# SiLU as one ScalarE function in a bottleneck-attention layer: Identity, Tanh and a VectorE product replaced, with table loads called for in advance

## The chip, the cores and the metric

The kernel runs on one core of a Trainium2 chip. The metric is the device time of one execution in microseconds (us). Five engines work side by side and wait for one another through semaphores: TensorE (PE in the profile, its weight loads on a line PEld), VectorE (DVE), ScalarE (ACT), GpSimd (POOL) and SyncE (SP), the last used here for DMA issue alone.

## The reference, cut to what matters

The input is x, 8 images of 512 channels and 32x32 pixels, float32. F = 32 is the side, C = 256, two bottlenecks (N = 2), 4 heads of 64.

```python
def cbs(x, w, p, pad):                       # convolution, batch norm, SiLU
    return silu(bn_eval(conv2d(x, w, pad), p))

t = cbs(gn(x), cv1_w, cv1_bn, 0)             # 512 -> 512 channels
ys = [t[:, :C], t[:, C:]]
for i in range(N):
    yi = ys[-1]
    z = cbs(yi, m_cv1_w[i], m_cv1_bn[i], 1)  # 3x3, 256 -> 256
    z = bot_attention(z, m_qkv_w[i], m_rw[i], m_rh[i])   # softmax(q (k+r)) v
    z = silu(bn_eval(conv2d(z, m_cv2_w[i], 0), m_cv2_bn[i]))
    ys.append(yi + z)
return x + cbs(concat(ys), cv2_w, cv2_bn, 0) # 1024 -> 512
```

gn is a group norm over 32 groups. silu(u) = u / (1 + exp(-u)). With h = u/2 that is h (1 + tanh h).

## The kernel before, in words

All 8 images are worked through by a loop that is written out (b = 0 to 7). A tile holds 128 channels (partitions) by 1024 pixels, and most instructions work on a half, 128x512. The framework lists the instructions of each engine in an order that follows the program text where nothing else decides, and each engine then takes its list strictly in that order. `tc.issue_after(ins)` only puts what its block creates on the engine of `ins` behind `ins` in that list.

One image has these stages, with the helper that does each:

- `cv1` (L652): four output tiles `oc`, each the product of 4 channel tiles, and SiLU of each half (L658). Two tiles go to `ypad`, the padded input of the 3x3 convolution, two to `y0`. For all images but the first this stage is done during the image before: the two `ypad` tiles by `first` and `second` (L809, L815) at the end of attention 0, the two `y0` tiles (L823) behind `m2`.
- `tiles_in` (L277): VectorE turns `ypad` into 6 sets of transformed tiles `v_in` (3 pairs of rows by 2 channel tiles; the last instruction of a set is L330).
- `conv3x3` (L660): for each of 2 output tiles, 3 groups of products on TensorE (L674), then `columns_out` (L334: one ScalarE copy into a tile with tag `h`, four VectorE instructions), `rows_out` (L343) and SiLU in place of the two halves of `z` (L684).
- `project` (L421): q, k and v from `z` (L272, L449), ScalarE copies of q (L435) and v (L454).
- `attention_fast` (L459): per group of 64 x 2 heads and half image, logits (L483), Exp on ScalarE (L487), sums on VectorE (L490, L492) and the product with v (L506); then ScalarE's copy L513 and VectorE's addition L514. A group's sums of exponentials (L523) are copied by ScalarE (L530) into tiles with the tags `h` and `t`. There are 8 Exps of 128x1024 in a group, 4 groups, 16 attentions.
- `m2` (L687): the second 1x1 product (L693), SiLU of four halves and the residual addition (L701) into `ypad[N]` or, in the second bottleneck, into `ylast`.
- `cv2` (L714): four output tiles of 8 channel tiles each, SiLU of 8 halves, the addition of x (L738) and the DMA of the result (L740), from a tile with tag `t`.

SiLU is made by `silu_parts` (L254): ScalarE's Identity takes the PSUM tile with a scale and a bias per channel into `h` (L258), ScalarE's Tanh takes `h` into `t` (L259), and VectorE multiplies (L264, L700 or L737 by the caller):

```python
nc.scalar.activation(h, ps, AF.Identity, scale=sh[:, k : k + 1], bias=bh[:, k : k + 1])
nc.scalar.activation(t, h, AF.Tanh)
nc.vector.scalar_tensor_tensor(dst, t, 1.0, h, ALU.add, ALU.mult)
```

The tags `h` and `t` have two buffers each; products go to a PSUM pool `big` with three. The scale `sh` and bias `bh` hold half of the batch norm's factors, so that h is u/2. Of the whole kernel 256 SiLU halves are made so. Weights of the 3x3 convolution are transformed during image 0 (`make_u`, L202, on VectorE and ScalarE) and read back from DRAM for the others (`load_u`). At the end a value decides whether a general version of the whole runs again (L873); with these inputs it does not.

Of the kernel before, what the change touches and what calls it, by code (L numbers as in the profile page):

```python
# [36 lines left out]
F32 = mybir.dt.float32  # L40
I32 = mybir.dt.int32
AF = mybir.ActivationFunctionType
ALU = mybir.AluOpType
# [4 lines left out]
P = 128  # L48
# [8 lines left out]
def kernel(  # L57
# [16 lines left out]
    nc = tc.nc  # L74
# [8 lines left out]
    HALF = 512  # L83
    NH = HW // HALF
    ROWS = HALF // F
    SCALE = HD**-0.5
# [4 lines left out]
    const = ctx.enter_context(tc.tile_pool(name="const", bufs=1))  # L91
    fast = ctx.enter_context(ExitStack())
    act = fast.enter_context(tc.tile_pool(name="act", bufs=1))
# [30 lines left out]
    def bn_slot(src, n):  # L124
        at = len(bn_chunks)
        for c in range(n):
            bn_chunks.append(src[ts(c, P), :])
        return at

    bn_cv1 = bn_slot(cv1_bn, NX)  # L130
    bn_m1 = [bn_slot(m_cv1_bn[n], NM) for n in range(N)]
    bn_m2 = [bn_slot(m_cv2_bn[n], NM) for n in range(N)]
    bn_cv2 = bn_slot(cv2_bn, NO)
    NBN = len(bn_chunks)
    bnp = const.tile([P, NBN, 4], F32, name="bnp")
# [42 lines left out]
        ypad.append(yp)  # L178


    sh = const.tile([P, NBN], F32, name="sh")
    bh = const.tile([P, NBN], F32, name="bh")
    rstd = const.tile([P, NBN], F32, name="rstd")
    nc.vector.tensor_scalar(rstd, bnp[:, :, 3], BN_EPS, None, ALU.add)
    nc.gpsimd.tensor_tensor(rstd, rstd, mhalf[:, :NBN], ALU.pow)
    nc.vector.scalar_tensor_tensor(sh, bnp[:, :, 0], 0.5, rstd, ALU.mult, ALU.mult)
    nc.vector.tensor_tensor(bh, bnp[:, :, 2], sh, ALU.mult)
    nc.vector.scalar_tensor_tensor(bh, bnp[:, :, 1], 0.5, bh, ALU.mult, ALU.subtract)

    for at in bn_m1:  # L190
        nc.vector.tensor_scalar(sh[:, at : at + NM], sh[:, at : at + NM], 1 / 48, None, ALU.mult)
# [56 lines left out]
    def inner(yp, c, half):  # L248
        return yp[:, c, 1 + half * ROWS : 1 + (half + 1) * ROWS, :].rearrange("p h w -> p (h w)")

    def stages(act, small, ps_big, ps_av, n_pt):


        def silu_parts(ps, k):  # L254

            h = act.tile([P, HALF], F32, tag="h", name="h", bufs=2)
            t = act.tile([P, HALF], F32, tag="t", name="t", bufs=2)
            nc.scalar.activation(h, ps, AF.Identity, scale=sh[:, k : k + 1], bias=bh[:, k : k + 1])  # L258
            nc.scalar.activation(t, h, AF.Tanh)  # L259
            return h, t  # L260

        def silu(dst, ps, k):
            h, t = silu_parts(ps, k)
            nc.vector.scalar_tensor_tensor(dst, t, 1.0, h, ALU.add, ALU.mult)  # L264

        def conv1x1(w_of, rhs_of, nk, ks=None, ps=None):

# [191 lines left out]
        def attention_fast(n, z, at, behind):  # L459
# [9 lines left out]
            pairs = [steps[i : i + PAIR] for i in range(0, len(steps), PAIR)]  # L469
            pts, accs, avs = {}, {}, {}  # L470

            def logits(pair):
                g, j0 = pair[0]
                c, half = groups[g]
                pt = act.tile([P, PAIR, 2, HALF], F32, tag="pt", name="pt", bufs=n_pt)
                pts[pair[0]] = pt
                for i, (_, j) in enumerate(pair):
                    ps = ps_big.tile([P, 2, HALF], F32, tag="big", name="l_ps")
                    for hd in range(2):
                        r = slice(hd * HD, (hd + 1) * HD)  # L480
                        for kh in range(2):
                            o = j * P + kh * HD
                            nc.tensor.matmul(  # L483
                                ps[kh * HD : (kh + 1) * HD, hd, :], kr[r, c, o : o + HD],
                                q[r, c, ts(half, HALF)], start=True, stop=True,
                            )
                    nc.scalar.activation(pt[:, i], ps, AF.Exp, scale=SCALE)  # L487
                if j0 == 0:
                    accs[g] = act.tile([P, 2, HALF], F32, tag="acc", name="acc", bufs=2)
                    return nc.vector.tensor_tensor(accs[g], pt[:, 0], pt[:, 1], ALU.add)  # L490
                for i in range(PAIR):
                    ins = nc.vector.tensor_tensor(accs[g], accs[g], pt[:, i], ALU.add)  # L492
                return ins
# [92 lines left out]
            ps, rows, s_dram = sums(g)  # L586
# [73 lines left out]
        def conv3x3(n, vs, u_of):  # L660
            z = act.tile([P, NM, HW], F32, tag="z", name="z")
            for oc in range(NM):
                us = u_of(oc)
                r = act.tile([P, 2, 2, NT * NW, 2], F32, tag="acc", name="r_mid", bufs=2)
                ends = act.tile([P, 2, NT * NW, 2], F32, tag="rs", name="r_ends", bufs=2)
                rs = (r[:, 0], r[:, 1], ends)
                flat = [a.rearrange("p r q o -> p r (q o)") for a in rs]
                first, last = rows_out(z[:, oc, :], *flat)
                for i in range(PAIRS):
                    ps = ps_big.tile([P, 2, NC, NT * NW], F32, tag="big", name="c3_ps")  # L670
                    for row in range(2):
                        for col in range(NC):
                            for k in range(NM):
                                nc.tensor.matmul(  # L674
                                    ps[:, row, col, :], us[i][:, k, row, col, :], vs[i][:, k, row, col, :],
                                    start=(k == 0), stop=(k == NM - 1),
                                )
                    columns_out(rs[i], ps)
                    if i == 1:
                        first()  # L680
                last()
                for half in range(NH):
                    part = z[:, oc, ts(half, HALF)]
                    silu(part, part, bn_m1[n] + oc)  # L684
            return z

        def m2(n, ao, yi, dst_of):  # L687

            pss = [ps_big.tile([P, NH, HALF], F32, tag="big", name="m2_ps") for _ in range(NM)]
            for half in range(NH):  # L690
                for oc in range(NM):
                    for k in range(NM):
                        nc.tensor.matmul(  # L693
                            pss[oc][:, half, :], m2_sb[:, n, k, ts(oc, P)], ao[:, k, ts(half, HALF)],
                            start=(k == 0), stop=(k == NM - 1),
                        )
            for half in range(NH):
                for oc in range(NM):
                    h, t = silu_parts(pss[oc][:, half, :], bn_m2[n] + oc)
                    nc.vector.scalar_tensor_tensor(t, t, 1.0, h, ALU.add, ALU.mult)  # L700
                    last = nc.vector.tensor_tensor(dst_of(oc, half), t, inner(yi, oc, half), ALU.add)  # L701
            return last

# [10 lines left out]
        def cv2(b, w2, ys, begun=None):  # L714


            def rows_of(dram, oc, half):
                if isinstance(b, int):
                    return dram[b, ts(oc, P), ts(half, HALF)]
                return dram[bass.ds(b, 1), ts(oc, P), ts(half, HALF)][0]  # L720

            def residual(oc, half):
                t = act.tile([P, HALF], F32, tag="xr", name="x_res", bufs=2)
                nc.gpsimd.dma_start(t, rows_of(x, oc, half))
                return t

            pieces = [(oc, half) for oc in range(NO) for half in range(NH)]
            res = [residual(*pieces[0]), residual(*pieces[1])]
            for i, (oc, half) in enumerate(pieces):
                if half == 0:  # L730
                    ks = range((2 + N) * NM)
                    if i == 0 and begun is not None:
                        ps = cv2_products(w2, ys, oc, ks[-NM:], begun)
                    else:
                        ps = cv2_products(w2, ys, oc, ks)
                h, t = silu_parts(ps[:, half, :], bn_cv2 + oc)
                nc.vector.scalar_tensor_tensor(t, t, 1.0, h, ALU.add, ALU.mult)  # L737
                nc.vector.tensor_tensor(t, t, res.pop(0), ALU.add)  # L738
                q = nc.sync if isinstance(b, int) and i + 2 >= len(pieces) and b == B - 1 else nc.gpsimd
                q.dma_start(rows_of(out, oc, half), t)  # L740
                if i + 2 < len(pieces):
                    res.append(residual(*pieces[i + 2]))
# [28 lines left out]
    for b in range(B):  # L771
# [3 lines left out]
        def u_of(n):  # L775
            def of(oc):
                if b == 0 and (oc, 0) not in us:
                    make_all(n, oc)
                return [us.pop((oc, i)) if (oc, i) in us else load_u(n, oc, i) for i in range(PAIRS)]

            return of
# [27 lines left out]
        def first():  # L809
            nonlocal nxt  # L810
            if more:
                nxt = new_y0()
                s.cv1(w1, xs, nxt, y1n, Y1S[: NM // 2])
# [133 lines left out]
```

## Time and profile before

| | us |
|---|---|
| median of 3 runs | 2662.72 (2661.3 to 2666.34) |
| the profiled execution's own time | 2659.74 |
| its span, from the first to the last instruction | 2658.2 |
| TensorE busy in it | 2469.9 |

The span is the time the rows below are counted in. The rest of the execution's own time, 1.54 us, lies around it. In a row of the timeline the first number is the start in us from the span's start, the second the length; xN means N instructions merged in one row; the brackets give the idle time of the engine before the row and what ended it.

### The profile page before, as it was taken

The numbers are of one execution on the slowest core, as the hardware profiler recorded it, in microseconds if no ns is written. First come the engines' busy times: TensorE is split into PE (matmuls) and PEld (weight loads), VectorE is DVE, ScalarE is ACT, GpSimd is POOL, SyncE is SP. The second block draws the span as 40 slices with busy tenths as digits, with TensorE's granted clock in tenths as the row PEclk, the third lists the DMA queues.
The fourth block names the chain that finished last, engine by engine and source line by source line (L and its number), as shares of the span: only waits on it lengthen the run. The fifth ranks groups of instructions, "written<-read, shape, count | busy, mean of one in ns | idle before, by whom it ended". The sixth has DMA issues, their size and how long they took to land. (4 is left out here: it accounts for less than half of the span.)

```text
span 2658.2 us, 36654 instructions
## 1 busy us (share of the span) xinstructions
PE 2469.9 (93%) x14626; PEld 1230.8 (46%) x14626; DVE 1673.7 (63%) x2780; ACT 1059.6 (40%) x1513; POOL 114.6 (4%) x378
## 2 busy tenths in 40 slices
PE   6788999989999899999999989999999999999798
PEld 3425436354463634536354353634536354363533
DVE  6678564775656665666665665657666675646753
ACT  2354432535234352353524434244442534325252
POOL 2000000000100001000010000100001000010000
PEclk9899999999999999999999999999999999999999
DMA  6123104040130302203031130502205011050101
GB/s 215 62 79 107 66 24 176 14 143 10 51 144 14 143 14 85 106 14 143 14 133 62 30 123 14 188 7 71 82 14 190 10 68 53 10 190 14 48 14 57
DMA packets 86195, 199.43 MB, mean 75 GB/s; under 512 B 32384, under 2 KB 42112, under 8 KB 73728
## 3 DMA queue, kind: packets, MB, share of 16 engines
q1 hardware_dynamic: 73696, 151.35, 16.6%
q0 software_dynamic: 12320, 45.66, 4.8%
q8 instruction: 117, 1.92, 0.3%
q14 instruction: 62, 0.51, 0.1%
HBM read 166.89 MB, written 30.08 MB: 74 GB/s over the span
## 5 line engine op out<-in xcount | busy, mean ns | idle before, releaser
L487 ACT ACTIVATE pt<-l_ps 128x1024 f32<-128x1024 f32 x512 | 496.3, 1025 | 228.7 <-PE l_ps L483 228.7
L492 DVE TENSOR_TENSOR acc<-acc,pt 128x1024 f32<-128x1024 f32 x384 | 469.8, 1223 | 147.6 <-ACT pt L487 123.8
L506 PE MATMUL av_ps<-pt,vT 64*64 64x512 f32 x4096 | 492.6, 596 | 12.3 <-DVE ao L514 10.9
L483 PE MATMUL l_ps<-q,kr 64*64 64x512 f32 x4096 | 498.4, 603 | 4.3 <-ACT pt L487 4.3
L674 PE MATMUL c_ps<-v_in,u 128*128 128x128 f32 x2688 | 313.6, 280 | 37.0 <-DVE v_in L330 27.5
L674 PEld LDWEIGHTS c_ps<-v_in,u 128*128 128x128 f32 x2688 | 310.8, 196 | 46.6 <-DVE v_in L330 30.0
L506 PEld LDWEIGHTS av_ps<-pt,vT 64*64 64x64 f32 x4096 | 155.1, 135 | 313.4 <-issue 227.3
L483 PEld LDWEIGHTS l_ps<-q,kr 64*64 64x64 f32 x4096 | 156.1, 135 | 290.5 <-issue 268.5
L272 PE MATMUL ps<-z,qkv_sb 128*128 128x512 f32 x512 | 245.5, 630 | 43.1 <-DVE z L264 43.1
L258 ACT ACTIVATE h<-ps,bh,sh 128x512 f32<-128x512 f32 x128 | 93.5, 774 | 367.6 <-PE ps L272 268.5
L272 PE MATMUL ps<-x,w 128*128 128x512 f32 x512 | 228.0, 602 | 2.2 <-DVE x L406 2.2
L272 PE MATMUL ps<-ypad,w 128*128 128x512 f32 x512 | 227.1, 594 | 0.0
L272 PEld LDWEIGHTS ps<-z,qkv_sb 128*128 128x128 f32 x512 | 100.6, 202 | 159.4 <-issue 103.4
L490 DVE TENSOR_TENSOR acc<-pt 128x1024 f32<-128x1024 f32 x64 | 78.4, 1225 | 138.4 <-ACT pt L487 138.4
L259 ACT ACTIVATE t<-h 128x512 f32<-128x512 f32 x256 | 149.7, 622 | 32.2 <-DMA out_dram<-t 24.2
L440 DVE TENSOR_TENSOR kr<-ps,rw_sb 128x512 f32<-128x512 f32 x64 | 41.2, 686 | 186.0 <-PE ps L272 186.0
L272 PEld LDWEIGHTS ps<-x,w 128*128 128x128 f32 x512 | 97.2, 192 | 130.9 <-issue 126.9
L272 PEld LDWEIGHTS ps<-ypad,w 128*128 128x128 f32 x512 | 96.6, 190 | 125.1 <-issue 125.1
L337 ACT COPY m<-c_ps 128x256 f32<-128x256 f32 x96 | 35.8, 373 | 243.1 <-PE c_ps L674 224.2
L737 DVE SCALAR_TENSOR_TENSOR t<-t,h 128x512 f32<-128x512 f32 x64 | 43.4, 695 | 139.7 <-ACT t L259 139.7
L530 ACT COPY s_row<-s_ps 128x512 f32<-128x512 f32 x128 | 68.7, 589 | 151.2 <-PE s_ps L523 148.7
L272 PE MATMUL ps<-ylast,w 128*128 128x512 f32 x256 | 117.2, 595 | 10.5 <-DVE ylast L701 10.5
(119 smaller groups left out, 2342.8 us busy)
## 6 DMA issues: line engine op xcount, KB each, us to landing
u<-u SPq DMA_DIRECT2D x84, 1024.0 KB
w<-in_cv_w_dram SPq DMA_DIRECT2D x24, 1024.0 KB
x<-in_x_dram SPq DMA_DIRECT2D x32, 512.0 KB
x_res<-in_x_dram POOLq DMA_DIRECT2D x64, 256.0 KB, 3.9
out_dram<-t POOLq DMA_DIRECT2D x62, 256.0 KB, 3.4
u<-u_new POOLq DMA_DIRECT2D x12, 1024.0 KB, 5.2
rs<-r_dram SPq DMA_DIRECT2D x96, 128.0 KB
raw<-in_m_cv_w_dram SPq DMA_DIRECT2D x8, 576.0 KB
```

The costliest lines, as they stand in the source:

```text
L258: nc.scalar.activation(h, ps, AF.Identity, scale=sh[:, k : k + 1], bias=bh[:, k : k + 1])
L259: nc.scalar.activation(t, h, AF.Tanh)
L272: nc.tensor.matmul(ps[:, half, :], w_of(k), rhs_of(k, half), start=(k == 0), stop=(k == nk - 1))
L440: nc.vector.tensor_tensor(dst, img(ps[:, half, :]), rw, ALU.add)
L483: nc.tensor.matmul(ps[kh * HD : (kh + 1) * HD, hd, :], kr[r, c, o : o + HD], q[r, c, ts(half, HALF)], start=True, stop=True,)
L487: nc.scalar.activation(pt[:, i], ps, AF.Exp, scale=SCALE)
L490: return nc.vector.tensor_tensor(accs[g], pt[:, 0], pt[:, 1], ALU.add)
L492: ins = nc.vector.tensor_tensor(accs[g], accs[g], pt[:, i], ALU.add)
L506: nc.tensor.matmul(avs[g][hd * HD : (hd + 1) * HD, kh, :], vT[r, j, o : o + HD], pt[r, i, hd, :], start=(j == 0), stop=(j == NJ - 1),)
L530: nc.scalar.copy(row, ps[:, kh, :])
L674: nc.tensor.matmul(ps[:, row, col, :], us[i][:, k, row, col, :], vs[i][:, k, row, col, :], start=(k == 0), stop=(k == NM - 1),)
L737: nc.vector.scalar_tensor_tensor(t, t, 1.0, h, ALU.add, ALU.mult)
```

## The change

SiLU becomes one ScalarE instruction with the scale and bias of the whole batch norm (no longer the half), straight into its target, or in `m2` and `cv2` into `t` with the addition behind. Two one-element-wide (128x1) ScalarE instructions are added per attention and convolution, Silu behind the last Exp of an attention and Exp behind the last Silu of a 3x3 convolution; the compiler puts a table load before an instruction whose function the loaded table does not hold. Copy and Identity are in every table.

```diff
+    spare = const.tile([P, 1], F32, name="spare")
+    zero = const.tile([P, 1], F32, name="zero")
+    nc.gpsimd.memset(zero, 0.0)
-    nc.vector.scalar_tensor_tensor(sh, bnp[:, :, 0], 0.5, rstd, ALU.mult, ALU.mult)
+    nc.vector.tensor_tensor(sh, bnp[:, :, 0], rstd, ALU.mult)
...
-        def silu_parts(ps, k):
...
-            nc.scalar.activation(h, ps, AF.Identity, scale=sh[:, k : k + 1], bias=bh[:, k : k + 1])
-            nc.scalar.activation(t, h, AF.Tanh)
-            return h, t
-        def silu(dst, ps, k):
-            h, t = silu_parts(ps, k)
-            nc.vector.scalar_tensor_tensor(dst, t, 1.0, h, ALU.add, ALU.mult)
+        def silu(dst, src, k):
+            return nc.scalar.activation(dst, src, AF.Silu, scale=sh[:, k : k + 1], bias=bh[:, k : k + 1])
+        def table_of(func):
+            nc.scalar.activation(spare, zero, func)
...
-                    nc.scalar.activation(pt[:, i], ps, AF.Exp, scale=SCALE)
+                    exp = nc.scalar.activation(pt[:, i], ps, AF.Exp, scale=SCALE)
+                if pair is pairs[-1]:
+                    with tc.issue_after(exp.ins):
+                        table_of(AF.Silu)
...
-                    silu(part, part, bn_m1[n] + oc)
+                    last_silu = silu(part, part, bn_m1[n] + oc)
+            with tc.issue_after(last_silu.ins):
+                table_of(AF.Exp)
...
-                    h, t = silu_parts(pss[oc][:, half, :], bn_m2[n] + oc)
-                    nc.vector.scalar_tensor_tensor(t, t, 1.0, h, ALU.add, ALU.mult)
+                    t = act.tile([P, HALF], F32, tag="t", name="t", bufs=2)
+                    silu(t, pss[oc][:, half, :], bn_m2[n] + oc)
...
-                h, t = silu_parts(ps[:, half, :], bn_cv2 + oc)
-                nc.vector.scalar_tensor_tensor(t, t, 1.0, h, ALU.add, ALU.mult)
+                t = act.tile([P, HALF], F32, tag="t", name="t", bufs=2)
+                silu(t, ps[:, half, :], bn_cv2 + oc)
```

## Rows read from the trace of the kernel before

**Rows 1.** The page, busy time of each engine, share of the span, instructions.
```profile
PE 2469.9 (93%) x14626; PEld 1230.8 (46%) x14626; DVE 1673.7 (63%) x2780; ACT 1059.6 (40%) x1513; POOL 114.6 (4%) x378
```
**Rows 2.** The waits: engine, line, released by: us in total, times, longest us.
```profile
PE ps L272 <- DVE z L264: 43.1, 16, 2.7
PE c_ps L674 <- DVE v_in L330: 32.2, 15, 2.9
...
ACT t L259 <- DMA out_dram<-t: 24.2, 17, 1.8
...
PE c_ps L674 <- ACT u_new L229: 19.1, 5, 7.1
...
PE ps L272 <- DVE ylast L701: 10.5, 8, 1.3
```
**Rows 3.** Groups by line and shape: busy us, mean ns | idle before.
```profile
L259 ACT ACTIVATE t<-h 128x512 f32<-128x512 f32 x256 | 149.7, 622 | 32.2 <-DMA out_dram<-t 24.2 <-DVE ylast L701 3.9 <-DVE ypad L701 3.4
...
L258 ACT ACTIVATE h<-z,bh,sh 128x512 f32<-128x512 f32 x64 | 48.5, 805 | 99.4 <-DVE z L366 99.4
...
L264 DVE SCALAR_TENSOR_TENSOR z<-t,h 128x512 f32<-128x512 f32 x64 | 41.4, 689 | 65.7 <-ACT t L259 65.6
...
L212 ACT ACT_TABLE_LOAD x1 | 1.3, 1283 | 1.0 <-PEq L933 1.0
```
**Rows 4.** Timeline of ACT, from a convolution's last SiLU to q's copy.
```profile
592.40 1.52 ACT L258 ACTIVATE h<-z,bh,sh 128x512 f32<-128x512 f32 x2 [3.33 <-DVE z L366]
593.82 1.13 ACT L259 ACTIVATE t<-h 128x512 f32<-128x512 f32 x2
598.95 1.07 ACT L435 COPY q<-ps 128x512 f32<-128x512 f32 x2 [4.00 <-PE ps L272]
```
**Rows 5.** Timeline of DVE and of PE in the same stretch.
```profile
594.47 1.29 DVE L264 SCALAR_TENSOR_TENSOR z<-t,h 128x512 f32<-128x512 f32 x2 [2.16 <-ACT t L259]
...
595.21 3.70 PE L272 MATMUL ps<-z,qkv_sb 128*128 128x512 f32 x8 [2.73 <-DVE z L264]
```
**Rows 6.** Timeline of PE: first and last restart of this kind that run longer.
```profile
443.40 5.40 PE L272 MATMUL ps<-z,qkv_sb 128*128 128x512 f32 x8 [2.72 <-DVE z L264]
...
2206.04 6.76 PE L272 MATMUL ps<-z,qkv_sb 128*128 128x512 f32 x8 [2.72 <-DVE z L264]
```
**Rows 7.** Stretches: us, PE, PEld, DVE, ACT, POOL busy (x), granted PE clock, DMA share, GB/s.
```profile
443.40:446.90 3.50, 3.50 (x5) 1.51 (x6) 0.91 (x2) 0.00 (x0) 0.00 (x0) 0.60 0.00 0
...
595.20:598.80 3.60, 3.59 (x9) 1.67 (x10) 2.13 (x4) 0.00 (x0) 0.00 (x0) 1.00 0.00 0
```
**Rows 8.** Timeline of ACT, DVE and PE, first bottleneck's m2 to the second convolution.
```profile
548.48 1.45 ACT L258 ACTIVATE h<-m_ps,bh,sh 128x512 f32<-128x512 f32 x2 [0.28 <-PE m_ps L693]
...
553.02 0.69 DVE L308 SCALAR_TENSOR_TENSOR w_tmp<-ypad 128x512 f32<-128x512 f32 x1
...
565.84 1.31 DVE L264 SCALAR_TENSOR_TENSOR y<-t,h 128x512 f32<-128x512 f32 x2
...
567.71 1.06 DVE L330 TENSOR_TENSOR v_in<-w_rows 128x512 f32<-128x512 f32 x1
...
568.83 3.84 PE L674 MATMUL c_ps<-v_in,u 128*128 128x128 f32 x32 [2.85 <-DVE v_in L330]
574.28 14.34 PE L674 MATMUL c_ps<-v_in,u 128*128 128x128 f32 x126 [1.62 <-DVE v_in L330]
```
**Rows 9.** Timeline of the second bottleneck's m2 and the start of cv2.
```profile
687.80 0.78 ACT L258 ACTIVATE h<-m_ps,bh,sh 128x512 f32<-128x512 f32 x1 [7.73 <-issue]
...
690.74 1.13 PE L272 MATMUL ps<-ylast,w 128*128 128x512 f32 x2 [1.31 <-DVE ylast L701]
```
**Rows 10.** Timeline of DVE, last image, first product of m2 to first row work.
```profile
2463.61 0.69 DVE L700 SCALAR_TENSOR_TENSOR t<-t,h 128x512 f32<-128x512 f32 x1 [2.74 <-ACT t L259]
...
2468.21 0.68 DVE L308 SCALAR_TENSOR_TENSOR w_tmp<-ypad 128x512 f32<-128x512 f32 x1
```
**Rows 11.** Timeline of ACT behind the last Exp of an attention.
```profile
526.50 0.59 ACT L513 COPY ao<-av_ps 128x512 f32<-128x512 f32 x1 [2.35 <-PE av_ps L506]
```

More of the change, by code (lines that the diff above doesn't have):

```diff
@@ L185 @@
     nc.gpsimd.tensor_tensor(rstd, rstd, mhalf[:, :NBN], ALU.pow)
-    nc.vector.scalar_tensor_tensor(sh, bnp[:, :, 0], 0.5, rstd, ALU.mult, ALU.mult)
+    nc.vector.tensor_tensor(sh, bnp[:, :, 0], rstd, ALU.mult)
     nc.vector.tensor_tensor(bh, bnp[:, :, 2], sh, ALU.mult)
-    nc.vector.scalar_tensor_tensor(bh, bnp[:, :, 1], 0.5, bh, ALU.mult, ALU.subtract)
+    nc.vector.tensor_tensor(bh, bnp[:, :, 1], bh, ALU.subtract)
     for at in bn_m1:
@@ L251, in stages @@
     def stages(act, small, ps_big, ps_av, n_pt):
-        def silu_parts(ps, k):
-            h = act.tile([P, HALF], F32, tag="h", name="h", bufs=2)
-            t = act.tile([P, HALF], F32, tag="t", name="t", bufs=2)
-            nc.scalar.activation(h, ps, AF.Identity, scale=sh[:, k : k + 1], bias=bh[:, k : k + 1])
-            nc.scalar.activation(t, h, AF.Tanh)
-            return h, t
-        def silu(dst, ps, k):
-            h, t = silu_parts(ps, k)
-            nc.vector.scalar_tensor_tensor(dst, t, 1.0, h, ALU.add, ALU.mult)
+        def silu(dst, src, k):
+            return nc.scalar.activation(dst, src, AF.Silu, scale=sh[:, k : k + 1], bias=bh[:, k : k + 1])
+        def table_of(func):
+            nc.scalar.activation(spare, zero, func)
         def conv1x1(w_of, rhs_of, nk, ks=None, ps=None):
```

## The prediction

> **What bounds the kernel now.** I read the page's busy times first. TensorE is busy for 93% of the span, VectorE for 63%, ScalarE for 40% [rows 1]. So a cheaper SiLU is worth something only where TensorE stands still for it; the busy time saved on ScalarE and VectorE is worth nothing by itself. Span less busy time leaves TensorE 188 us idle, and the second view, the waits, says for whom [rows 2]. Three of its rows have SiLU in the chain: TensorE waits 43.1 us in all, once in each of the 16 attentions, for the product L264 that finishes z; 32.2 us for v_in, VectorE's transform of the convolution's input; 10.5 us for ylast. A fourth, 19.1 us for u_new, is image 0's weight transform, which shares VectorE with SiLU. The third view, the groups, prices the instructions [rows 3], and the timeline shows who stands behind whom at each seam [rows 4 to 11].
>
> **What goes.** 256 Tanhs (149.7 us of ScalarE) and 256 VectorE products of about 0.69 us [rows 3], some 176 us of VectorE. What stays is one ScalarE instruction with the operands that Identity has now. No row shows a Silu. The bounds are Tanh's 0.62 us and the sum of both instructions, 0.81 + 0.62 = 1.43 us [rows 3]; I take Identity's 0.81 (0.78 from PSUM [rows 9]), the nearest row, since it takes the same two per-channel operands on the same shape.
>
> **Seam A, convolution to projection.** ScalarE runs Identity twice, then Tanh twice, and only then comes the first product [rows 4, 5]. It starts at 594.47, takes 0.69, and TensorE restarts at 595.21, 0.05 later. With Silu the first half is ready at 592.40 + 0.81 = 593.21, so the restart is at 593.26: 1.95 us earlier. The second half is ready at 592.40 + 1.52 = 593.92. TensorE's eight records take 3.70 us, two for each product, so it asks for that half some 0.86 us after the restart, at 594.12: no new wait. 16 x 1.95 = 31.2 us. At 1.43 us for a Silu, the second half would decide and the gain be about 0.9 us each, 14 us in all.
>
> **The clock behind seam A.** After this wait the eight records take 3.70 us at a granted clock of 1.00, or longer: 5.40 us in the first case, where the clock over the first 3.5 us is 0.60, a mix of 2.4 and 1.2 GHz [rows 5 to 7]. Of the 16 restarts 9 are long: six at 5.40, two at 5.20, and the last at 6.76 [rows 6]. Excess: 6 x 1.70 + 2 x 1.50 + 3.06 = 16.3 us. Of the wait of 2.72 us about 0.77 stays. The nearest shorter wait, 1.31 us ahead of cv2, is followed by two records in 1.13 us, which is full speed [rows 9], and so it is in all 8 images. So I take all 16.3; the bounds are 0 and 16.3.
>
> **Seam B, m2 of the first bottleneck to the second convolution, images 1 to 6.** VectorE runs without a pause from L308 at 553.02 until the set of v_in at 567.71 that ends TensorE's wait of 2.85 us; a second wait of 1.62 follows [rows 8]. In that stretch five SiLU products go (one of m2, and the four of y, two of which stand at 565.84), each 0.60 us in sequence: 3.0 us. It also starts earlier: the second and third Identity of m2 run from 548.48 [rows 8], so the third Silu ends at about 549.95, its addition 0.69 later, and L308 can start at about 550.65 instead of 553.02. Together 5.3 us, against 2.85 + 1.62 = 4.47 us of waiting. Both waits go: 6 x 4.47 = 26.8 us. If VectorE started no earlier, 3.0 a stage or 18 would be left.
>
> **Image 0.** The second convolution has a first wait of the same 2.85 us, which goes by the same sum. The weight transform of each convolution's second output tile runs on VectorE behind two products of z: 2 x 0.60 us, twice. Together 2.85 + 2.4 = 5.3 us; bounds 0 and 2.85 + 19.1 [rows 2].
>
> **Last image.** With no cv1 to cover it, TensorE waits for the whole chain. VectorE's four m2 products stand ahead of L308 at 2468.21, and the first waited for a Tanh [rows 10]: 4 x 0.61 + 0.63 = 3.1 us.
>
> **Seam C, m2 to cv2.** Identity, Tanh, product, addition take from 687.80 to 690.74 [rows 9]. Without Tanh and product they are 1.3 us shorter, all of the wait: 8 x 1.31 = 10.5 us [rows 2]. With a Silu at 1.40 it would be half.
>
> **Tail.** The last output tile's chain sheds one Tanh and one product: 1.3 us.
>
> **What is added.** A table load takes 1.28 us; the only row is at the start of the kernel [rows 3]. There will be one at the first Silu of image 0 and two per attention, 33 more. The 128x1 instruction has no row; its bounds are 0 and 0.59 us, the 128x512 copy [rows 11]. So a load with its caller costs 1.28 to 1.87 us. The Silu table is loaded behind the last Exp of an attention, where ScalarE idles 2.35 us until L513, which waits for TensorE [rows 11]; should that cover be gone, L513 and then the last group's addition are late. The Exp table is loaded behind z's last Silu at 593.92. Next comes q's copy, at 598.95 now, at 597.00 with TensorE moved forward by 1.95: 3.1 us of cover, and behind it TensorE has the v products to do. Cost on the path: 0 for both, at most 16 x (1.28 + 1.28) = 41 us if neither were covered. Image 0's first load stands beside cv1's products, which have three PSUM tiles: 0.
>
> The two instructions on VectorE that become a plain product, and the memset on POOL at the start, change nothing. The additions in m2 and cv2 stay.
>
> A wait moves: Tanh waits 24.2 us in all, 17 times, up to 1.8, for the DMA that empties a `t` buffer [rows 2]. Identity had then already emptied the PSUM tile; Silu will hold it. Behind it on ScalarE stand the other halves' Silus, and TensorE waits only if it wants that PSUM tile back. One output tile of cv2 is 32 records of 0.43 us, 13.7 us, and there are three PSUM buffers: 0, at most 24.2.
>
> The Trainium skill ("ScalarE: Activation LUTs", section Rules for kernel authors) speaks against the change: do all of one table set before switching, and budget about 2.7 us for every switch to a different set. By that, an estimate from the page, 33 switches are 89 us of ScalarE; if all lay on the path, the sum would be a gain of about 6 us. The one row here has 1.28 us, with nothing close enough behind it to show a longer hold.
>
> **Sum.** 31.2 + 16.3 + 26.8 + 5.3 + 3.1 + 10.5 + 1.3 = 94.5 us. The profiled execution took 2659.74, so 2565.2; the median shown is 2.98 above it, so I predict 2568 us (-3.6%).
>
> **Rivals.**
> 1. *Half the terms only.* The clock still falls after the shorter wait, VectorE starts no earlier in seam B, or a Silu costs more than Identity. For it: 9 of 16 long restarts among nearly equal waits show that the length of the wait alone does not decide. Against: the full-speed restarts after 1.31 us. With no clock gain, 18 in seam B and nothing in image 0: 94.5 - 16.3 - 8.8 - 5.3 = 64.1, time 2599.
> 2. *The loads lie on the path,* because the calls do not bring them forward or the load holds ScalarE longer than rows 3 say. 94.5 - 41 = 53.5, time 2609. Against: the idle times of 2.35 and 4.00 us, and that TensorE does not need ScalarE in either at once. By the page's price the time would be about 2657.
> 3. *Slower: Silus slip between Exps.* cv1's first four halves per image now need no VectorE instruction and no `h` and `t` buffers, so nothing but TensorE's order keeps them behind the last Exps. Each one between two Exps costs two loads, 2.57 us, and stops TensorE long enough for a restart at the lower clock, 1.70 us more. All 28 (7 images) are 120 us: time 2662.7 + 120 - 94.5 = 2688. It decides from 23 of them on. Against: their products stand behind the attention's last logits in TensorE's list, and ScalarE is through with its last Exp before L513 [rows 11], with no Identity between Exps now.
>
> **How the numbers follow.** Forecast, 2568 and within some 17 us of it: 0.62. Rival 1, about 2585 to 2608: 0.24. Rival 2: 0.05. Rival 3: 0.04. A larger gain, where image 0's 19.1 us go too and TensorE is not held up elsewhere, below 2551: 0.03. A new wait that eats all but 5 us: 0.02. The low end of the range is the sum with a Silu at Tanh's 0.62 us (16 x 0.19 = 3 more) and most of image 0's wait (15 more): 2550. The high end is rival 1 with a Silu at its upper bound in part of the seams: 2608. A measurement of this kernel can tell about 0.2%, 5 us, from no change. Faster by more: 0.93; within: 0.03; slower: 0.04.
>
> **What would show it.** In the changed profile: 34 table loads in all, none between Exps; TensorE's wait for z at about 0.8 us, named after ScalarE, and restarts of 3.70 us; the waits for v_in gone except in the last image; the wait for ylast gone; ScalarE busy about 960 us (1059.6 less 149.7, plus 33 loads of 1.28 and 32 calls of some 0.3) and VectorE about 1500 (1673.7 less 176). I am wrong if a Silu's row is far from 0.8 us, if L513 or q's copy starts late behind a load, if TensorE's wait for z stays near 2.7, or if new waits of similar total appear in attention.

## The result and the profile after

The changed kernel takes 2545.36 us (median of 4 runs, 2543.0 to 2547.56) beside 2662.2 us for the kernel before: a ratio of 0.9558, 95% interval 0.9541 to 0.9575. That is 4.4% faster, where 3.6% was predicted, and 4.6 us below the low end of the range. The profiled execution took 2544.53 us with a span of 2543.0, against 2658.2 before, so 115.2 us went, where the steps summed to 94.5.

The page's busy times after the change, to be held against [rows 1]:

```profile
PE 2436.7 (96%) x14626; PEld 1213.0 (48%) x14626; DVE 1521.0 (60%) x2524; ACT 966.6 (38%) x1322; POOL 115.0 (5%) x379
```

ScalarE and VectorE came out at 967 and 1521 us where about 960 and 1500 were foreseen, and their own 93 and 153 us do not add to the gain as such. Look at TensorE instead: with the same 14,626 instructions its busy time fell by 33.2 us, and its idle time (span less busy) from 188.3 to 106.3, by 82.0. The first is in the main the clock: the same instructions of the same shapes took less time, and the mean granted clock rose from 0.976 to 0.989.

TensorE's waits after the change, against [rows 2] (engine, line, released by: us in total, times, longest us):

```profile
PE gm_ps L379 <- DVE mv L374: 21.1, 7, 3.1
...
PE c_ps L677 <- ACT u_new L233: 9.3, 3, 6.5
PE ps L272 <- ACT z L260: 7.3, 16, 0.5
...
PE ps L272 <- ACT t L260: 4.3, 8, 0.5
...
PE c_ps L677 <- DVE v_in L330: 3.6, 2, 2.0
```

The 43.1 us for z are 7.3 and end with ScalarE; v_in's 32.2 are 3.6, in the last image alone; u_new's 19.1 are 9.3; ylast is gone and a new wait of 8 times some 0.5 us stands in its place.

Groups after the change (line engine op, out<-in, shapes, count | busy us, mean ns | idle before), against [rows 3]:

```profile
L260 ACT ACTIVATE z<-z,bh,sh 128x512 f32<-128x512 f32 x64 | 48.6, 805 | 87.4 <-DVE z L366 87.4
L264 ACT ACT_TABLE_LOAD x32 | 41.1, 1283 | 0.6
L264 ACT ACTIVATE spare<-zero 128x1 f32<-128x1 f32 x32 | 6.5, 203 | 0.4
...
L677 PE MATMUL c_ps<-v_in,u 128*128 128x128 f32 x2688 | 305.4, 276 | 10.3 <-issue 6.6 <-DVE v_in L330 3.6
L272 PE MATMUL ps<-z,qkv_sb 128*128 128x512 f32 x512 | 229.3, 595 | 7.3 <-ACT z L260 7.3
L677 PE MATMUL c_ps<-v_in,u_new 128*128 128x128 f32 x384 | 49.7, 293 | 14.0 <-ACT u_new L233 9.3 <-DVE r_ends L341 3.0 <-DVE r_mid L341 1.5
```

A Silu costs what Identity cost, 805 ns, to the nanosecond. The 128x1 call takes 203 ns. 32 loads stand at the calls, 2 more at L216 and at image 0's first Silu: 34, as counted. For the last three rows the kernel before has this:

```profile
L674 PE MATMUL c_ps<-v_in,u 128*128 128x128 f32 x2688 | 313.6, 280 | 37.0 <-DVE v_in L330 27.5 <-issue 9.6
L272 PE MATMUL ps<-z,qkv_sb 128*128 128x512 f32 x512 | 245.5, 630 | 43.1 <-DVE z L264 43.1
...
L674 PE MATMUL c_ps<-v_in,u_new 128*128 128x128 f32 x384 | 53.6, 306 | 25.0 <-ACT u_new L229 19.1 <-DVE v_in L330 4.8 <-DVE u_tmp L226 1.1
```

Each row holds two of the gains apart: what its idle time lost is a wait, and what its busy time lost is low clock. The group with u_new is image 0's two convolutions.

Seam A after the change, ScalarE and then TensorE (start, length, what, [idle before <- releaser]), against [rows 4, 5]:

```profile
565.15 1.52 ACT L260 ACTIVATE z<-z,bh,sh 128x512 f32<-128x512 f32 x2 [3.01 <-DVE z L366]
566.69 1.28 ACT L264 ACT_TABLE_LOAD   x1
567.98 0.20 ACT L264 ACTIVATE spare<-zero 128x1 f32<-128x1 f32 x1
569.75 1.07 ACT L435 COPY q<-ps 128x512 f32<-128x512 f32 x2 [1.57 <-PE ps L272]
...
566.02 3.70 PE L272 MATMUL ps<-z,qkv_sb 128*128 128x512 f32 x8 [0.46 <-ACT z L260]
```

The first half is ready at 565.15 + 0.81 = 565.96 and TensorE restarts at 566.02; the second half comes in time, for the eight records stay together. The Exp table is loaded directly behind the last Silu, and ScalarE then still waits 1.57 us before q's copy: the cover held. All 16 restarts are 3.70 us.

Seam B after the change, TensorE, against [rows 8]: one row for a whole convolution, with no pause in it.

```profile
540.09 21.60 PE L677 MATMUL c_ps<-v_in,u 128*128 128x128 f32 x192
```

The Silu load behind an attention's last Exp, ScalarE, against [rows 11]:

```profile
500.28 1.94 ACT L487 ACTIVATE pt<-l_ps 128x1024 f32<-128x1024 f32 x2 [1.37 <-PE l_ps L483]
502.24 1.28 ACT L264 ACT_TABLE_LOAD   x1
503.53 0.20 ACT L264 ACTIVATE spare<-zero 128x1 f32<-128x1 f32 x1
504.57 0.59 ACT L516 COPY ao<-av_ps 128x512 f32<-128x512 f32 x1 [0.84 <-PE av_ps L509]
```

Load and call take 1.5 us of the 2.35 that ScalarE idled there, and 0.84 is left.

### The profile page after: what moved, and what is told of

Same layout as the page of the kernel before. It is cut to its first block, busy times and chain, and to the rows that moved or that the text cites. A ratio compares the mean times of both kernels' runs of the same rounds, so it can differ in the third digit from the quotient of the medians.

```text
span 2543.0 us, 35923 instructions
## 1 busy us (share of the span) xinstructions
PE 2436.7 (96%) x14626; PEld 1213.0 (48%) x14626; DVE 1521.0 (60%) x2524; ACT 966.6 (38%) x1322; POOL 115.0 (5%) x379
## 4 chain that ended last, share of the span: by engine, by line
PE 81%; DVE 8%; ACT 4%; issue 2%; DMA 1%; SPq 0%; ACTq 0%; POOL 0%; DVEq 0%
PE ps L272 31%; PE av_ps L509 14%; PE l_ps L483 13%; PE c_ps L677 12%; PE m_ps L698 4%; PE v_ps L449 4%; ACT pt L487 3%; PE s_ps L526 2%; DVE acc L495 1%; DVE ao L517 1%; DVE st L373 1%; DMA rs<-r_dram 1%; ACT t L260 1%; ACT z L260 1%; DVE r_ends L364 0%
## 5 line engine op out<-in xcount | busy, mean ns | idle before, releaser
L509 PE MATMUL av_ps<-pt,vT 64*64 64x512 f32 x4096 | 491.4, 595 | 12.6 <-DVE ao L517 11.2
L483 PE MATMUL l_ps<-q,kr 64*64 64x512 f32 x4096 | 493.7, 597 | 4.3 <-ACT pt L487 4.3
L677 PE MATMUL c_ps<-v_in,u 128*128 128x128 f32 x2688 | 305.4, 276 | 10.3 <-issue 6.6
L677 PEld LDWEIGHTS c_ps<-v_in,u 128*128 128x128 f32 x2688 | 304.5, 193 | 18.0 <-issue 13.6
L272 PE MATMUL ps<-z,qkv_sb 128*128 128x512 f32 x512 | 229.3, 595 | 7.3 <-ACT z L260 7.3
L260 ACT ACTIVATE t<-ps,bh,sh 128x512 f32<-128x512 f32 x64 | 47.1, 775 | 310.6 <-PE ps L272 190.8
L743 DVE TENSOR_TENSOR t<-t,x_res 128x512 f32<-128x512 f32 x64 | 43.9, 692 | 181.9 <-ACT t L260 155.9
L272 PEld LDWEIGHTS ps<-z,qkv_sb 128*128 128x128 f32 x512 | 94.7, 190 | 114.1 <-issue 91.8
L272 PE MATMUL ps<-y,w 128*128 128x512 f32 x256 | 118.0, 599 | 4.3 <-ACT t L260 4.3
```

The source lines that it names most:

```text
L260: return nc.scalar.activation(dst, src, AF.Silu, scale=sh[:, k : k + 1], bias=bh[:, k : k + 1])
L272: nc.tensor.matmul(ps[:, half, :], w_of(k), rhs_of(k, half), start=(k == 0), stop=(k == nk - 1))
L483: nc.tensor.matmul(ps[kh * HD : (kh + 1) * HD, hd, :], kr[r, c, o : o + HD], q[r, c, ts(half, HALF)], start=True, stop=True,)
L509: nc.tensor.matmul(avs[g][hd * HD : (hd + 1) * HD, kh, :], vT[r, j, o : o + HD], pt[r, i, hd, :], start=(j == 0), stop=(j == NJ - 1),)
L677: nc.tensor.matmul(ps[:, row, col, :], us[i][:, k, row, col, :], vs[i][:, k, row, col, :], start=(k == 0), stop=(k == NM - 1),)
```

## The experiments

Theory: the gain is made of (a) a shorter chain to z, (b) VectorE's freed time and shorter m2 chains ahead of the second convolution, and (c) TensorE's clock, which falls less often because the long waits for z and v_in are gone; the table loads lie beside other work. The rivals were that the loads cost something even so, that VectorE's load has no part in it, and that the clock's gain has nothing to do with the length of the waits. Eight kernels tell these apart.

**Which SiLUs pay.** `e3_z_only` uses Silu for the 64 halves of z and the old form for the other 192; `e4_not_z` is the reverse. Both have the calls. e3 is the kernel before with them, with whole factors for z, and z has:

```diff
-                    silu(part, part, bn_m1[n] + oc)
+                    k = bn_m1[n] + oc
+                    last_silu = nc.scalar.activation(part, part, AF.Silu, scale=sh[:, k : k + 1], bias=bh[:, k : k + 1])
```

and in e4, the changed kernel with z's factors halved again:

```diff
-                    last_silu = silu(part, part, bn_m1[n] + oc)
...
+                    nc.scalar.activation(h, part, AF.Identity, scale=sh[:, k : k + 1], bias=bh[:, k : k + 1])
+                    last_silu = nc.scalar.activation(t, h, AF.Tanh)
+                    nc.vector.scalar_tensor_tensor(part, t, 1.0, h, ALU.add, ALU.mult)
```

> Silu only for z, the 64 halves behind the 3x3 convolutions, with the calls; the other 192 halves keep Identity, Tanh and the product. My theory (the chain ahead of the projection and the low clock behind it): 16 x 2.26 = 36 us of waiting and 16 us of clock, ratio 0.980 (2610 us). Rival (VectorE's freed time carries the gain, in proportion to the products removed): a quarter of 117 = 29 us, ratio 0.989.

> The complement: Silu for the 192 halves of cv1, m2 and cv2, with the calls; z keeps Identity, Tanh and the product. My theory: 117 - 52 = 65 us, ratio 0.976 (2597 us), with TensorE still waiting 2.7 us for z each time and 9 of 16 restarts long. Rival (proportion of products): three quarters, 88 us, ratio 0.967.

Measured: 2601.22 us, 0.976 (0.9744 to 0.9776), and 2600.49 us, 0.976 (0.9744 to 0.9776). Groups of e3:

```profile
L685 PE MATMUL c_ps<-v_in,u 128*128 128x128 f32 x2688 | 317.4, 282 | 32.2 <-DVE v_in L338 22.6 <-issue 9.6
L280 PE MATMUL ps<-z,qkv_sb 128*128 128x512 f32 x512 | 229.3, 595 | 7.3 <-ACT z L696 7.3
```

and of e4:

```profile
L678 PE MATMUL c_ps<-v_in,u 128*128 128x128 f32 x2688 | 305.2, 276 | 10.4 <-issue 6.6 <-DVE v_in L331 3.8
L273 PE MATMUL ps<-z,qkv_sb 128*128 128x512 f32 x512 | 241.1, 621 | 43.0 <-DVE z L693 43.0
```

Each part brings 2.4%, which is 58.3 us (e3) and 59.3 us (e4) by the spans of the profiled executions; together that is 117.6, against 115.2 for the whole, so the two gains add. By the medians, held against a higher median of the kernel before (2664.46), they are 63 and 64. For e4 that is what was expected; e3 gained more than the 0.980 expected and far more than the rival's quarter. The rows come apart cleanly: who keeps a wait keeps the low clock behind it. With Silu for z alone the z group drops to 229.3 us busy and the convolutions keep 317.4; with Silu everywhere else the convolutions drop to 305.2 and z keeps 241.1. So the convolutions have a low-clock term of their own, 8 to 12 us, which the prediction does not contain.

**The length of the wait and the clock.** `e5_delay1` and `e6_delay2` put one and two in-place ScalarE copies of a z tile ahead of the last two Silus, so that the wait at seam A grows and VectorE is left as it is:

```diff
+                    for _ in range(1 if oc == NM - 1 and half == 0 else 0):
+                        nc.scalar.copy(z[:, oc, :], z[:, oc, :])
```

(2 in place of 1 in e6.)

> The changed kernel with one ScalarE copy of z in place (128x1024, about 1.0 us) ahead of the last two Silus of each convolution: the wait for z grows from 0.46 to about 1.5 us, VectorE's work stays. My theory (a wait of this length does not bring the low clock): 16 x 1.05 = 17 us, 2562 us, ratio 0.962, and restarts of 3.70 us. Rival (each longer wait costs a low clock too): up to 16 x 1.7 = 27 us more, ratio 0.972.

> The same with two copies: the wait for z is about 2.5 us, near the 2.7 of the kernel before. My theory (half of the gain that I had not counted is clock, and it comes back with the length of this wait alone): 16 x 2.1 = 34 us and 10 to 30 us of long restarts, 2590 to 2610 us, ratio 0.973 to 0.980. Rival (the low clock went because of the other waits): 34 us and no long restart, 2579 us, ratio 0.969.

Measured: 2564.34 us, 0.9637 (0.9612 to 0.9661), and 2599.31 us, 0.9767 (0.9742 to 0.9791). A restart of TensorE in e5:

```profile
567.80 3.70 PE L272 MATMUL ps<-z,qkv_sb 128*128 128x512 f32 x8 [1.53 <-ACT z L260]
```

and two in e6:

```profile
573.52 5.40 PE L272 MATMUL ps<-z,qkv_sb 128*128 128x512 f32 x8 [2.61 <-ACT z L260]
742.97 3.70 PE L272 MATMUL ps<-z,qkv_sb 128*128 128x512 f32 x8 [2.61 <-ACT z L260]
```

The first copy lengthens the wait by 17.3 us over the 16 attentions, and the span by 19.0; every restart stays at 3.70. The second adds 17.2 more, but 32.6 to the span: 7 of the 16 restarts are now 5.40, and TensorE's busy time is 14.5 us up. So after a wait of 1.5 us no restart ran slow, after 2.6 us about half did, and the second microsecond of waiting costs nearly twice the first. Equal waits of 2.61 end in either form; what decides between them within one kernel these runs do not show.

**VectorE's part.** `e7_dve_back` gives VectorE its 256 products back, off every chain, into a tile that nobody reads:

```diff
-            return nc.scalar.activation(dst, src, AF.Silu, scale=sh[:, k : k + 1], bias=bh[:, k : k + 1])
+            ins = nc.scalar.activation(dst, src, AF.Silu, scale=sh[:, k : k + 1], bias=bh[:, k : k + 1])
+            nc.vector.scalar_tensor_tensor(side, dst, 1.0, dst, ALU.add, ALU.mult)
+            return ins
```

> The changed kernel with VectorE's 256 products back, from each Silu's output into a tile that nobody reads: VectorE has its old work and its place in the order, but neither TensorE nor ScalarE waits for the product itself. My theory (z and ylast gain by the shorter chain, v_in by VectorE's time): the waits for v_in come back in part, 6 x 2.2 us, and some 5 us in image 0, ratio 0.962 to 0.966 (2560 to 2572 us). Rival (VectorE's freed time carries the gain): 0.99 to 1.0.

Measured: 2583.57 us, 0.9712 (0.968 to 0.9744), 37.4 us of span more than the changed kernel. Its waits:

```profile
PE c_ps L680 <- DVE v_in L333: 27.2, 17, 1.7
...
PE c_ps L680 <- ACT u_new L234: 17.2, 5, 6.0
...
PE ps L275 <- ACT z L261: 7.3, 16, 0.5
```

The time comes back where VectorE's order is the bound, v_in 23.6 us and u_new 7.9 us more, and nowhere at z. The timeline shows the products standing in the middle of the transform, VectorE and then TensorE:

```profile
554.16 0.69 DVE L262 SCALAR_TENSOR_TENSOR side<-y 128x512 f32<-128x512 f32 x1
...
557.13 3.84 PE L680 MATMUL c_ps<-v_in,u 128*128 128x128 f32 x32 [1.55 <-DVE v_in L333]
562.60 14.34 PE L680 MATMUL c_ps<-v_in,u 128*128 128x128 f32 x126 [1.63 <-DVE v_in L333]
```

So about a third of the gain (37 of 115) is VectorE's freed time, more than I had expected; the rest is shorter chains and the clock. An engine that is busy for 65% of the span here still set TensorE's start in this one stage.

**The table loads.** `e1_no_calls` is the changed kernel without the two calls; `e2_calls_only` is the kernel before with them, so that 31 tables are loaded for nothing.

```diff
-                if pair is pairs[-1]:
-                    with tc.issue_after(exp.ins):
-                        table_of(AF.Silu)
...
-            with tc.issue_after(last_silu.ins):
-                table_of(AF.Exp)
```

> The changed kernel without the 128x1 calls: the loads then stand right in front of the first Silu and the first Exp that need them. My theory (the loads are hidden either way, except where ScalarE is late at the start of an attention): the Silu load runs while ScalarE waits for TensorE and costs nothing; the Exp load falls between q's copy and the first Exps, where ScalarE has about 0.4 us to spare, so 16 x 0 to 1.3 us: ratio to the kernel before 0.956 to 0.963 (2545 to 2564 us). Rival (the calls carry the change): 16 x 2 x 1.28 = 41 us and more at the low clock, ratio 0.971 or above.

> The kernel before with nothing but the 128x1 calls at the places where the change puts them, so 32 loads are added while Identity, Tanh and the product stay. My theory: all loads lie beside TensorE's work, ratio 1.000 (0.998 to 1.002). Rival (a switch costs 1.28 us or more on the path): +41 us, ratio 1.015.

Measured: e1 2573.43 us, 0.9651 (0.9632 to 0.967); e2 2663.06 us, 0.9994 (0.9982 to 1.0006). In e2 ScalarE is busy for 1105.4 us instead of 1059.6, and the time does not move beyond the interval, some 0.1%: a load in these two places costs nothing that can be measured here. In e1 there are just as many loads, but they stand where somebody waits. The timeline of e1, ScalarE and TensorE at the first Exp, then ScalarE at m2 of the second bottleneck:

```profile
444.21 1.07 ACT L435 COPY q<-ps 128x512 f32<-128x512 f32 x2 [5.79 <-PE ps L272]
445.30 1.28 ACT L487 ACT_TABLE_LOAD   x1
446.59 3.77 ACT L487 ACTIVATE pt<-l_ps 128x1024 f32<-128x1024 f32 x4
...
447.67 1.09 PE L483 MATMUL l_ps<-q,kr 64*64 64x512 f32 x8 [0.76 <-ACT pt L487]
...
664.60 1.28 ACT L260 ACT_TABLE_LOAD   x1 [7.71 <-issue]
665.90 1.45 ACT L260 ACTIVATE t<-m_ps,bh,sh 128x512 f32<-128x512 f32 x2
```

At the first Exp TensorE has filled its PSUM tiles with logits and stops for 0.76 us, 16 times. At m2 the load stands behind the wait for m_ps and not in it: ScalarE idled 7.71 us, and only then loaded, so the Silu is 1.28 us late and cv2 with it (8 waits for ylast, 9.6 us). The span is 29.0 us longer. TensorE idles 21.4 us of that, 12.8 more in waits for the first Exp and 5.3 more ahead of cv2. The other 7.6 us are busy time, and they do not stand behind these pauses: all 16 restarts after 0.76 us take 1.09 us for eight records, at a granted clock of 1.00 (447.67), and cv2's first records take 1.12. They lie in attention (l_ps, av_ps and s_ps are 4.9, 1.9 and 0.9 us busier). Over half is low clock behind gm_ps's wait, which is 21.1 us in both kernels: 6 of its 7 restarts are long in e1, 4 of 7 in the changed kernel. The rest is in image 0. No row ties these 7.6 us to the calls. By the two ratios e1 is 0.9% slower, some 25 us. The calls are thus worth more than I had expected, though less than the rival said: without them the change brings 3.5%.

These rows also price a switch. From the copy's end at 445.28 to the start of the Exp at 446.59 it is 1.31 us: the load's 1.28, and nothing behind it. The Trainium skill ("ScalarE: Activation LUTs", section What ACT_TABLE_LOAD costs) gives the same 1283 ns for the load, and adds a drain that brings every switch to about 2.66 us. The first figure agrees, the sum does not: no switch shown here holds ScalarE for more than 1.31 us, and the measurement decides.

**A version that goes on.** With SiLU's waits gone, the longest in the list is gm_ps, 7 times 3.0 us: the next image's group mean, in the middle of an attention. `e8_mean_later` moves it one attention group later, where its statistics are long done:

```diff
             stats(range(NX // 2, NX))
+            yield
             gm, dev = gn_mean(mv)
             yield
             gr = gn_rstd(dev)
-            apply(range(NX // 2), gm, gr)
-            yield
-            yield apply(range(NX // 2, NX), gm, gr)
+            yield apply(range(NX), gm, gr)
```

> The changed kernel with the next image's group-norm mean one attention group later and the whole normalization in the last group, so that TensorE does not stand 3.09 us before it for VectorE's statistics. My theory: 7 x 3.0 = 21 us of waiting and about 8 us of low clock behind it go, 2517 us, ratio 0.945. Rival (the normalization then comes too late for cv1, and TensorE waits there): ratio 0.956 or above.

Measured: 2523.3 us, 0.9478 (0.9454 to 0.9501), below both kernels and 6 us above the expected 2517. TensorE in the changed kernel, and then in this one:

```profile
461.75 0.56 PE L379 MATMUL gm_ps<-mv,gmat 128*128 128x4 f32 x2 [3.09 <-DVE mv L374]
462.24 3.69 PE L483 MATMUL l_ps<-q,kr 64*64 64x512 f32 x16
465.71 3.05 PE L509 MATMUL av_ps<-pt,vT 64*64 64x512 f32 x16
```

```profile
476.19 0.39 PE L379 MATMUL gm_ps<-mv,gmat 128*128 128x4 f32 x2
476.51 1.95 PE L482 MATMUL l_ps<-q,kr 64*64 64x512 f32 x16
478.27 1.90 PE L508 MATMUL av_ps<-pt,vT 64*64 64x512 f32 x16
```

The wait goes (21.1 us in all), and so does the low clock behind it: the 16 records behind the mean take 1.95 instead of 3.69 us, the next 16 take 1.90 instead of 3.05, and TensorE's busy time falls by 7.5 us. Against that stand 3.3 us more waiting for ao and 3.0 more for pt; the span is 20.4 us shorter.

## Why the prediction was right and wrong

The direction held, and most of the waits went for the reasons given; the sum came out 20.7 us short, mostly by clock that it left out. Term by term, from the idle and the busy time of the groups of both kernels:

| step of the prediction | predicted, us | measured, us | from |
|---|---|---|---|
| Seam A, the wait | 31.2 | 35.8 | idle of the z group, 43.1 less 7.3 |
| The clock behind seam A | 16.3 | 16.2 | its busy time, 245.5 less 229.3 |
| Seam B and Last image, the waits | 26.8 + 3.1 | 26.7 | idle of c_ps<-v_in,u, 37.0 less 10.3 |
| Image 0, the waits | 5.3 | 11.0 | idle of c_ps<-v_in,u_new, 25.0 less 14.0 |
| Seam C | 10.5 | 6.2 | wait for ylast 10.5, new wait 4.3 |
| Tail | 1.3 | 2.3 | see below |
| What is added: loads, calls, moved wait | 0 | 0 | e2 |
| low clock behind v_in and u_new | not in the sum | 12.1 | busy, 313.6 less 305.4 and 53.6 less 49.7 |
| low clock in attention | not in the sum | 5.9 | busy, l_ps 498.4 less 493.7, av_ps 492.6 less 491.4 |

The rows add to 116.2; the other groups of TensorE, and what overlaps between groups, come to 1.0 the other way, and 115.2 is what went.

**The step that failed is "The clock behind seam A".** Its own size came out at 16.2 us for 16.3, but that is one execution, from whose trace both numbers were read: behind the same waits the z group has 24.6 us above its 229.3 in e2 and 11.8 in e4. What was wrong is that it was the only clock term, and that its bound, 16.3, was taken as the bound of all the clock could give: TensorE's busy time fell by 33.2 us, twice that, of which 12.1 stood behind v_in and u_new. A low clock can follow any wait of that length, and the prediction itself names these two kinds, v_in's 2.85 us and u_new's up to 7.1, but priced them as waits alone. None of its own signs of being wrong came up: they ask for the price of a Silu, for waits and for starts, and not for TensorE's busy time. The timeline and the stretches (us, PE, PEld, DVE, ACT, POOL busy, granted clock, DMA share, GB/s) of the kernel before would have told:

```profile
1212.74 20.86 PE L674 MATMUL c_ps<-v_in,u 128*128 128x128 f32 x158 [2.84 <-DVE v_in L330]
```

```profile
1212.74:1216.74 4.00, 4.00 (x18) 4.00 (x19) 4.00 (x11) 0.00 (x0) 0.17 (x2) 0.50 0.61 256
...
568.83:572.67 3.84, 3.83 (x32) 3.64 (x32) 3.84 (x11) 0.19 (x1) 0.17 (x2) 1.00 0.64 262
```

After equal waits the restart at 568.83 [rows 8] ran at 2.4 GHz and the one at 1212.74 at half of it, a clock of 0.50. I had read the first and multiplied it by six. In two of the six images (1212.74 and 1858.05) the slow restart swallows the second wait of 1.62 us, so that the wait term there is 4 x 4.47 + 2 x 2.85 = 23.6 and not 26.8, and some 2.7 us each (20.86 less 3.84 and 14.34) hide in the busy time. The last image, predicted at 3.1, lost 3.3: its first wait went from 9.59 to 6.60 us, and one of 0.31 is gone. Together that is the 26.7 measured, within rounding. The rival "Half the terms only" had the clock wrong the other way: it has the shorter wait leave the clock low, and all 16 restarts are at 3.70.

**Seam A** was 4.6 us too small. A rest of 0.77 was expected and 0.46 is left, 16 times. Silu began 0.08 us before TensorE ran dry in the kernel before (592.40 against 595.21 - 2.73) and begins 0.41 before it now (565.15 against 566.02 - 0.46): the transform ahead of it ends earlier. VectorE no longer stands 2.16 us in front of a Tanh in the middle of it, behind the first output tile, where the kernel before has:

```profile
583.49 1.29 DVE L264 SCALAR_TENSOR_TENSOR z<-t,h 128x512 f32<-128x512 f32 x2 [2.16 <-ACT t L259]
```

That fits, and VectorE's freed time is not it: e7 gives the products back, and its wait for z is 7.3 all the same. No run isolates the Tanh.

**Seam B** was right in its mechanism: both waits go in images 1 to 6, and e7 shows that VectorE's order was the cause. **Image 0** was sized from z's products and one v_in alone. In e3, with Silu for z only, its wait for u_new falls from 19.1 to 16.9, close to the 2.4 of that argument; in e4, with the others only, to 10.4. So most of it belongs to the other SiLUs, cv1's and m2's, which I had left out; that they kept VectorE from the weight transforms is not shown by a row. The prediction had a larger gain through image 0, below 2551 us, at a chance of 0.03. The time came out there, but only partly by that way: image 0's waits gave 5.7 us more than their term, the clock beyond seam A 18.0, of which 5.9 can't be given to the change.

**Seam C** gave 6.2 of 10.5. The timeline of the changed kernel ahead of cv2, TensorE and then ScalarE:

```profile
660.15 1.13 PE L272 MATMUL ps<-ylast,w 128*128 128x512 f32 x2
661.81 1.12 PE L272 MATMUL ps<-y,w 128*128 128x512 f32 x2 [0.54 <-ACT t L260]
...
660.32 2.32 ACT L260 ACTIVATE t<-m_ps,bh,sh 128x512 f32<-128x512 f32 x3 [0.94 <-PE m_ps L698]
```

and ScalarE in the kernel before:

```profile
689.47 1.45 ACT L258 ACTIVATE h<-m_ps,bh,sh 128x512 f32<-128x512 f32 x2 [0.23 <-PE m_ps L693]
```

TensorE no longer waits for ylast at 660.15. But two records later it begins cv2's next output tile, and of the three PSUM tiles it needs the one that m2's third half still holds. The Silu that reads it is the second of the three that begin at 660.32, and by their durations it ends some 1.45 us later, at 661.77. In the kernel before the Identity in its place ended at 689.47 + 1.45 = 690.92, and TensorE, held up by ylast until 690.74, did not ask for the tile before 691.71. So this wait was always there behind the other one; "all of the wait" looked at what is late now and not at what is late next. In e1 and e7, where ylast is late again, its row is gone.

The moved wait that "What is added" weighed, for the buffer of cv2's result, grew from 24.2 to 119.9 us, and TensorE never stops for it: 0, as put. Its reasoning was off: Identity had not always emptied the PSUM tile, but waited itself for VectorE's product to free `h`. Before and after:

```profile
ACT h L258 <- DVE t L737: 99.1, 14, 12.2
```

```profile
ACT t L260 <- DMA out_dram<-t: 119.9, 14, 15.3
```

So 99.1 + 24.2 = 123.3 us became 119.9: the wait was there before, mostly under another name.

**Tail**: the last addition ended 4.4 us behind TensorE's last product before, at 2652.29 behind 2647.87, and 2.1 us now, at 2537.36 behind 2535.27. So 2.3 us went: both halves' Tanhs and products stood in line, not one.

**What is added** held, but for that reasoning: 34 loads, none between Exps, the Silu's price, both covers. The third rival (slower) needed Silus between Exps; there are none. The second lost with e2, and the price that the Trainium skill gives with the rows of e1. The low clock in attention is the one term I cannot give to the change: gm_ps waits 21.1 us before and after, all 7 restarts behind it are long before and 4 after, and the busy time of l_ps is 498.6, 498.6, 496.1 and 494.2 us in e1, e2, e4 and e7; e8 shows where most of it lies.

## What to carry to other kernels

Price a wait of the bounding engine together with the clock behind it, for every group that restarts after such a wait and not only for the one where it was noticed: the busy time of a group, held against its fastest equal (595 ns a record here, against 630), shows it in one row. Shortening a wait of 2.6 us by 1 us was worth nearly 2 us in this kernel (e6 against e5). And a function that needs another table cost nothing measurable where its load was called for in an idle stretch of ScalarE, while the load stood behind the wait, not in it, where it was left to the first instruction that needs it.

## What was not expected of the hardware

The clock after a wait is not a function of the wait alone: within e6, 16 waits of 2.61 us were followed by 7 restarts of 5.40 us and 9 of 3.70. A restart at half clock can cost less than it shows, where the engine would have waited again: at 1212.74 in the kernel before, 158 records took 20.86 us, and at 568.83 the same 158 took 19.79 with their second wait, so 1.07 us were lost and not 2.7. A table load waits with the instruction it belongs to, even where ScalarE has been idle for 7.71 us (e1). And a restart after a wait of some 3 us is not always slow: behind gm_ps, whose wait is the same in every kernel but e8, from 4 to 7 of the 7 restarts were long.
